# Between two scans: channels split 128 and 64, means through GpSimd, convolution by halves

## The chip, the cores and the metric

The kernel runs on one core of a Trainium2 chip. The metric is the device time of one execution in microseconds; a version's time is the median of its runs. For the kernel before it is 23751.5 us (three runs, 23744.67 to 23764.05). Times inside the kernel come from one profiled execution.

## The reference

The input is x with eight images of 64 x 64 positions and 192 channels, all fp32. Two layers follow each other. Each normalises its input by groups of channels and adds its result to it. The change lies in the second one:

```
x = x + L1(gn(x))
L1:  xc, z = split(x @ in_proj.T)            # 384 channels each
     xc = silu(depthwise_conv3x3(xc) + b)
     xs = xc by rows, by columns, and both reversed        # 4 directions
     dt, B, C = xs @ x_proj ;  delta = softplus(dt @ dt_proj + bias)
     h = exp(delta * A) * h + delta * B * xs ;  y = sum_n h * C     # scan over 4096 positions
     y = sum of the four directions + xs * D
     y = layernorm(y) * silu(z) ;  return y @ out_proj.T
```

## The kernel before, in words

Layer 0 comes first, for all images, and leaves its result channel-major in DRAM (x1s). Layer 1 (function layer1) then takes one image after the other. Positions go in eight tiles of TT = 512 (eight rows of the image); the 384 inner channels are DT = 3 groups of 128 partitions; the 192 outer channels are CT = 2 groups of CP = 96 partitions.

The scan of an image (function scan, its part main) is written out in a fixed order and is not touched. Between the scan of image b-1 and that of image b stands a boundary, which does two things side by side: the finish of image b-1, and the front of image b with the prologue of its scan. The loop over b at the end of layer1 runs nine times: the first boundary has only a front, the last only a finish.

The front (function front) loads a tile of x1s, projects it with p_x (L1141, two matmuls that add over the two groups of 96 channels) into a PSUM bank, copies it with a bias into a padded image (pad, L1171), and convolves: ScalarE writes tap 0 (L1192), VectorE adds taps 1 to 8 with scalar_tensor_tensor in place over the whole image, 128 x 4096 (L1202). Then ScalarE applies SiLU by halves (L1215) and writes the result three ways to DRAM: by channels (L1220), transposed by columns (xt, L1230 and L1234), and by tokens (by_tokens: four TensorE transposes p_xq, a copy xq, a DMA; L1249 to L1261). When all is written, the prologue may load (xc, ut; L1462 and L1466), project (p_d), make the step widths (spa, de), transpose (p_du) and weigh (pw, L1592); then decays ea and transposes g feed the first scans.

The finish (function finish) works on yacc, the sum of the four directions, which stays in SBUF as 128 x 3 x 4096. By tile: the mean over 384 channels is three matmuls with a matrix of 1/384 (p_m, L1281), VectorE subtracts it (L1289), ScalarE squares (L1299), three matmuls give the variance (p_v, L1281), ScalarE takes logarithm and exponential (L1317, L1318), VectorE multiplies (L1324), ScalarE scales and shifts by group (L1331). Beside it z is projected from a reloaded tile of x1s (p_z, L1361) and goes through SiLU (L1379); VectorE multiplies (L1391), p_o projects to 192 channels (L1408), VectorE adds the input (L1417), and a DMA stores.

The order on each engine is not written by hand. The class Flow is a planner: each piece of front and finish is a generator of steps with an engine, a guessed cost and buffers to take and give. At each turn Flow issues the step that could start first by its guesses (a rank breaks ties), and keeps that order on every engine with order-only dependencies. The guesses never reach the chip; the order does. Two waits are thus to be kept apart: a generator's wait orders the plan, while on the chip an engine runs its queue in order and waits by semaphores for data and buffers. All DMAs are issued by SP.

PSUM in a boundary: five banks mm (means, p_z, p_o, prologue), two banks fx (p_x, p_xq), one outside. SBUF buffers: two xl1, two xs, one xt, two xq; three xl2, two z, one square. The scan's own buffers h1 (hs, hc) take memory that the finish leaves.

Of the kernel before, what the change touches and what calls it, by code (L numbers as in the profile page):

```python
# [8 lines left out]
F32 = mybir.dt.float32  # L9
# [84 lines left out]
class Flow:  # L94
# [48 lines left out]
    def start(self, req, ready):  # L143
# [3 lines left out]
        if req[0] == "take":  # L147
            return (-1.0, max(ready, min(self.slots[req[1]]))) if self.slots[req[1]] else None
# [6 lines left out]
    def run(self):  # L155
        while self.chains:
# [8 lines left out]
            if req[0] == "take":  # L165
                self.slots[req[1]].remove(min(self.slots[req[1]]))
# [866 lines left out]
def layer1(tc, consts, x1s, mv1, out, w_in, w_x, w_dt, w_out):  # L1033
# [5 lines left out]
    image = lambda ap: ap.rearrange("(t p) l -> p t l", p=CP)  # L1039

    with ExitStack() as ctx:
# [8 lines left out]
        wi = wp.tile([CP, CT, 2 * DIN], F32, name="wi1")  # L1050
        nc.sync.dma_start(out=wi, in_=w_in.rearrange("(t p) m -> p t m", p=CP))
# [25 lines left out]
        sc, sh = gn_affine(tc, sp, mp, mv1.rearrange("p b t s -> p (b t) s"), grp, eps)  # L1077
        pb = mp.tile([128, TT], F32, name="p_gb", tag="mm")
        for m in range(2 * DT):
            for ct in range(CT):  # L1080
                nc.tensor.matmul(
                    pb[:, m * nb : m * nb + nb],
                    wi[:, ct, m * 128 : m * 128 + 128],
                    sh.rearrange("p (b t) -> p b t", t=CT)[:, :, ct],
                    start=ct == 0,
                    stop=ct == 1,
                )
# [5 lines left out]
        def scaled(w, b, half):  # L1093

            for ct in range(CT):
# [5 lines left out]
                            w[:, ct],  # L1101
                            wi[:, ct, half * DIN : half * DIN + DIN],
                            AF.Copy,
                            scale=sc[:, b * CT + ct : b * CT + ct + 1],
# [5 lines left out]
        def front(f, cx, mq, b, xo):  # L1110


            fp = cx.enter_context(tc.tile_pool(name="fr1", bufs=1, reuse_waits="tile"))
            wx_b = fp.tile([CP, CT, DIN], F32, name="wx1b")
            pads = [fp.tile([128, HI + 2, WI + 2], F32, name=f"pad{i}") for i in range(2)]
            for tag, n in (("xl", 2), ("fx", 2), ("pad", 2), ("xs", 2), ("xt", 1), ("xq", 2)):
# [3 lines left out]
            def load():  # L1120
                for d in range(DT):
                    for t in range(NT):
                        tk = slice(t * TT, t * TT + TT)
                        yield "take", "xl"
                        xl = got["xl", d, t] = fp.tile([CP, CT, TT], F32, name="xl1", bufs=2)
                        r = yield step("SP", 0.1, lambda: [nc.sync.dma_start(out=xl, in_=image(x1s[b])[:, :, tk])])
                        f.at["xl", d, t] = r + 3

            def project():
                yield from scaled(wx_b, b, 0)  # L1130
                for d in range(DT):
                    for t in range(NT):
                        yield "wait", ("xl", d, t)
                        xl = got["xl", d, t]
                        yield "take", "fx"
# [758 lines left out]
```

## Time and profile before

| what | us |
|---|---|
| median of three runs | 23751.5 |
| profiled execution, its own time | 23759.13 |
| its span | 23757.4 |
| first stretch without a scan (front alone) | 196.2 |
| seven boundaries with front and finish | 251.3, 248.6, 248.0, 247.2, 248.1, 248.5, 248.6 |
| last stretch (finish alone) | 135.5 |
| a scan between two boundaries (5070.0 to 7173.6) | 2103.6 |

A stretch is counted from the end of one scan's last hc (L1648 on GpSimd) to the start of the next scan's first. The profile's page has one line per group of instructions: line, engine, operation, output and inputs with shapes, count; then busy time and mean duration, and the idle time of the engine just before them with what ended it. In a table of stretches each engine has its busy microseconds and, in brackets, its instructions; then come the granted clock of TensorE, the share of the DMA engines, and GB/s. An fp32 matmul stands in the trace as two instructions.

### The profile page before, as it was taken

How to read it: one execution, taken by the hardware profiler on the slowest of the kernel's cores; microseconds unless marked ns; L12 is line 12 of the kernel's file. 1: busy time of each engine (PE TensorE's matmuls, PEld its weight loads, DVE VectorE, ACT ScalarE, POOL GpSimd, SP SyncE). 2: the span in 40 equal slices, each digit the busy share in tenths (PEclk: the TensorE clock that was granted, in tenths of full speed). 3: DMA queues.
4: the chain of work that ended last, by engine and by line, in shares of the span. 5: the costliest groups of instructions: out<-in, count | busy, mean ns of one | idle time of the engine just before them, and what ended most of it. 6: DMA issues, size and time to landing. Idle time of an engine off the chain costs nothing.

```text
span 23757.4 us, 313126 instructions
## 1 busy us (share of the span) xinstructions
PE 21089.6 (89%) x100804; PEld 10279.5 (43%) x100804; DVE 21274.2 (90%) x22093; ACT 21040.0 (89%) x37507; POOL 16067.4 (68%) x12871
## 2 busy tenths in 40 slices
PE   7999999978888888888888888888888888888888
PEld 4444444434444444444444444444444444444444
DVE  7888888779998999899989998999899989998998
ACT  5666766669998999899989998999899989998998
POOL 1111111149995999599959985998699769976997
PEclk8999999989999999999999999999999999999999
DMA  2111111133233323333233233323332233233332
GB/s 50 45 44 44 46 44 43 39 99 81 81 79 107 81 82 78 107 81 82 76 112 81 82 77 109 81 81 79 110 82 81 78 107 82 81 85 100 82 83 67
DMA packets 1368290, 1859.75 MB, mean 78 GB/s; under 512 B 268576, under 2 KB 697024, under 8 KB 1357440
## 3 DMA queue, kind: packets, MB, share of 16 engines
q1 hardware_dynamic: 1366656, 1839.73, 28.7%
q8 instruction: 810, 13.27, 0.2%
q14 instruction: 824, 6.75, 0.1%
HBM read 1225.98 MB, written 210.50 MB: 60 GB/s over the span
## 4 chain that ended last, share of the span: by engine, by line
POOL 43%; PE 24%; ACT 15%; DVE 7%; issue 6%; DMA 4%; SPq 1%; POOLq 0%; ACTq 0%; DVEq 0%
POOL hc L1648 40%; ACT pw L1592 6%; ACT ea L1607 6%; POOL cy L1646 3%; PE p_f L956 3%; DMA xc<-xo 2%; DVE xs L1202 2%; PE p_f L976 2%; PE p_x L448 2%; PE y L1663 2%; PE p_o L873 2%; PE p_y L790 1%; PE g L1618 1%; PE p_d L1481 1%; PE p_z L531 1%
## 5 line engine op out<-in xcount | busy, mean ns | idle before, releaser
L1648 POOL TENSOR_TENSOR hc<-hs,cb 128x1024 f32<-128x1024 f32 x6144 | 14592.9, 2375 | 12.0 <-POOL cy L1646 9.9
L1634 DVE TENSOR_TENSOR_SCAN hs<-ea,cy,g 128x512 f32<-128x512 f32 x10752 | 13024.0, 1262 | 608.6 <-PE g L1618 411.1
L1592 ACT ACTIVATE pw<-duT,bt 128x384 f32<-128x384 f32 x16384 | 8874.1, 601 | 20.2 <-DVE duT L1539 20.2
L1607 ACT ACTIVATE ea<-dr,an 128x512 f32<-128x512 f32 x12288 | 8120.5, 709 | 189.2 <-DVE hs L1634 170.8
L1663 PE MATMUL y<-hc,sel 128*64 128x512 f32 x24576 | 6624.0, 617 | 1841.3 <-POOL hc L1648 1819.2
L1618 PEld LDWEIGHTS g<-ident,pw 128*128 128x128 f32 x49152 | 5288.7, 141 | 4336.8 <-issue 2671.4
L1618 PE MATMUL g<-ident,pw 128*128 128x128 f32 x49152 | 6788.4, 279 | 60.1 <-ACT pw L1592 28.6
L1646 POOL COPY cy<-hs 128x2 f32<-128x2 f32 x6144 | 1164.2, 189 | 3373.5 <-DMA out_x<-xl 1733.8
L1663 PEld LDWEIGHTS y<-hc,sel 128*64 128x64 f32 x24576 | 1225.9, 134 | 3254.1 <-POOL hc L1648 3031.3
L1634 DVE TENSOR_TENSOR_SCAN hs<-ea,g 128x512 f32<-128x512 f32 x1536 | 1763.7, 1202 | 159.0 <-PE g L1618 115.6
L365 POOL TENSOR_TENSOR s<-xs 96x512 f32<-96x512 f32 x64 | 121.1, 1892 | 2033.7 <-DVE xs L343 1522.9
L1202 DVE SCALAR_TENSOR_TENSOR xs<-pad,p,xs 128x4096 f32<-128x4096 f32 x192 | 860.9, 4484 | 43.4 <-ACT xs L1192 36.2
L1510 PE MATMUL p_dt<-xdbl,wd 13*128 13x512 f32 x1536 | 857.2, 639 | 41.0 <-DVE de L1523 39.1
L365 POOL TENSOR_TENSOR s<-sq 96x512 f32<-96x512 f32 x128 | 211.6, 1653 | 964.1 <-ACT sq L378 899.8
L1481 PE MATMUL p_d<-xc,wx 128*44 128x512 f32 x1536 | 791.6, 598 | 22.6 <-DMA xc<-xo 22.0
L343 DVE SCALAR_TENSOR_TENSOR x<-xx,p,x 96x512 f32<-96x512 f32 x1024 | 785.2, 815 | 19.4 <-ACT x L332 19.4
L956 PE MATMUL p_f<-h,wf 96*128 96x512 f32 x1536 | 761.9, 632 | 24.4 <-ACT zs L550 14.0
L343 DVE SCALAR_TENSOR_TENSOR xs<-xin,p,xs 96x512 f32<-96x512 f32 x1024 | 749.3, 767 | 4.6 <-ACT xs L332 4.6
L976 PE MATMUL p_f<-m,wf 128*96 128x512 f32 x1536 | 692.9, 601 | 0.0
L1532 PEld LDWEIGHTS p_du<-ident,de 128*128 128x128 f32 x3072 | 323.5, 141 | 610.2 <-DVE de L1523 405.8
L448 PE MATMUL p_x<-h,wi 96*128 96x512 f32 x1024 | 544.5, 664 | 12.3 <-ACT h L405 11.1
L365 POOL TENSOR_TENSOR s<-x 96x512 f32<-96x512 f32 x64 | 96.2, 1502 | 626.3 <-DVE x L343 477.2
(202 smaller groups left out, 19557.2 us busy)
## 6 DMA issues: line engine op xcount, KB each, us to landing
cb<-cd SPq DMA_DIRECT2D x4096, 128.0 KB
dr<-de SPq DMA_DIRECT2D x3072, 128.0 KB
xc<-xo SPq DMA_DIRECT2D x256, 768.0 KB
e<-csd SPq DMA_DIRECT2D x256, 384.0 KB
xl<-x SPq DMA_DIRECT2D x256, 384.0 KB
ut<-xo SPq DMA_DIRECT2D x128, 768.0 KB
ut<-xo SPq DMA_DIRECT2D x256, 384.0 KB
xo<-xs SPq DMA_DIRECT2D x48, 1024.0 KB
```

The source lines that it names most:

```text
L343: nc.vector.scalar_tensor_tensor(im(out[:, ct]), tap(ct, j), w[:, ct, j : j + 1], im(out[:, ct]), ALU.mult, ALU.add)
L956: nc.tensor.matmul(ps, wf1[:, ct, mt * 128 : mt * 128 + 128], h[:, ct], start=ct == 0, stop=ct == 1)
L976: nc.tensor.matmul(ps[:CP], wf2[:, kt, ct * CP : ct * CP + CP], m[:, kt], start=kt == 0, stop=kt == 5)
L1202: nc.vector.scalar_tensor_tensor(xs, tap(j), kw[:, d, j : j + 1], xs, ALU.mult, ALU.add)
L1481: nc.tensor.matmul(st["p_d"][:44], wx[:, d, k], st["xc"][:, d], start=d == 0, stop=d == DT - 1)
L1592: nc.scalar.activation(st["pw", p, j][:, :, i], st["duT"][:, j].rearrange("p (g c) -> p g c", c=64), AF.Copy, scale=st["bt"][:, j, n : n + 1],
L1607: nc.scalar.activation(ea[:, f], state[s]["dr", d][:, f], AF.Exp, scale=an[:, k, p, at : at + 1])
L1618: nc.tensor.transpose(g[:, f, j * 128 : j * 128 + 128], state[s]["pw", p, j][:, 2 * d + f].rearrange("p a b -> p (a b)"), ident,)
L1634: nc.vector.tensor_tensor_scan(rev(h[:, f]), rev(ea[:, f]), rev(g[:, f]), 0.0 if first(s) else state[s - 1]["cy"][:, p, d, f : f + 1], ALU ...
L1646: o(nc.gpsimd.tensor_copy(st["cy"][:, p, d], h[:, :, last]))
L1648: o(nc.gpsimd.tensor_mul(hc, h, bc(st["cb", p], 1, [128, 2, TT])))
L1663: o(nc.tensor.matmul(y[half[f]], sel, hc[:, f], start=p == 0 and k > 0, stop=p == NP1 - 1))
```

## The change

It rewrites the boundary and leaves layer 0 and the scan alone.

- Outer channels are held as 128 partitions and 64 (twice, once on each half of the partitions) instead of 96 and 96. Two tiles of 512 go together: a load is three DMAs (parts), a projection is pair: two matmuls over 128 channels, then two over 64 channels, one on each half of the array's rows. The output projection does 128 columns a tile, and the other 64 columns of both tiles side by side on halves of the array's columns (rest). Scale and shift of the group norm are moved to that layout through DRAM once (affd, aff).
- The mean over 384 channels: GpSimd adds the three groups (two additions of 128 x 512 into ys, one buffer), then one matmul instead of three.
- The convolution runs in two halves of 32 rows with three xs buffers; SiLU, stores, tokens and the transposing copy follow by halves.
- PSUM: mm has three banks, p_z two of its own (zz). A pair of p_x takes both fx banks, a pair of p_z both zz banks.
- The plan: LATE makes centre and gate wait, from tile 4 on, for the first tap of the last convolution's halves; every chain has a rank, LAG is 0.35 and RANK 1.0; a take may ask for several buffers.
- The softplus of the step widths (spa: exp, then ln with a bias of 1) is the same in both files.

```diff
+    def parts(ap, xl, t):
+        two = ap.rearrange("c (t l) -> c t l", l=TT)[:, t : t + 2]
+        return [(xl[:, 0:2], two[0:128])] + [(xl[i * 64 : i * 64 + 64, 2], two[128:C, i]) for i in range(2)]
+    def pair(w, m, ps, xl):
+        out = [nc.tensor.matmul(ps[i], w[:, 0, m], xl[:, i], start=True, stop=False) for i in range(2)]
+        for i in range(2):
+            rows = slice(i * 64, i * 64 + 64)
+            out.append(nc.tensor.matmul(ps[i], w[rows, 1, m], xl[rows, 2], start=False, stop=True))
+        return out
...
+        affd = dp.tile([C, 2, nb], F32, name="affd", bufs=1)
+        aff = wp.tile([128, 2, 2, nb], F32, name="aff")
+        for i, a in enumerate((sc, sh)):
+            for ct in range(CT):
+                nc.sync.dma_start(
+                    out=affd[ct * CP : ct * CP + CP, i], in_=a.rearrange("p (b t) -> p t b", t=CT)[:, ct]
+                )
+        nc.sync.dma_start(out=aff[:, 0], in_=affd[0:128])
+        for i in range(2):
+            nc.sync.dma_start(out=aff[i * 64 : i * 64 + 64, 1], in_=affd[128:C])
...
             def convolve():
                 for d in range(DT):
-                    yield "wait", ("pad", d)
-                    xs = got["xs", d] = fp.tile([128, HI, WI], F32, name="xs1", bufs=2)
-                    tap = lambda j: pads[d % 2][:, j // 3 : j // 3 + HI, j % 3 : j % 3 + WI]
+                    for h in range(2):
+                        yield "wait", ("pad", d, h)
+                        xs = got["xs", d, h] = fp.tile([128, HI // 2, WI], F32, name="xs1", bufs=3)
+                        at = h * HI // 2
+                        tap = lambda j: pads[d % 2][:, at + j // 3 : at + j // 3 + HI // 2, j % 3 : j % 3 + WI]
...
-                    xt = fp.tile([128, WI, HI], F32, name="xt1")
-                    r = yield step("ACT", 7.2, lambda: [nc.scalar.copy(xt, xs.rearrange("p h w -> p w h"))])
+                            lambda: [nc.scalar.copy(xt[:, :, at : at + HI // 2], xs.rearrange("p h w -> p w h"))],
...
-            def mean(ps, src):
-                return [nc.tensor.matmul(ps, on, src[:, d], start=d == 0, stop=d == DT - 1) for d in range(DT)]
+            def mean(src):
+                yield "take", "ys"
+                ys = fp.tile([128, TT], F32, name="ys", bufs=1)
+                yield step(
+                    "POOL",
+                    2.6,
+                    lambda: [nc.gpsimd.tensor_add(ys, src[:, 0], src[:, 1]), nc.gpsimd.tensor_add(ys, ys, src[:, 2])],
+                )
+                yield "take", "mm"
+                ps = mq.tile([128, TT], F32, name="p_m", tag="mm")
+                r = yield step("PE", 1.0, lambda: [nc.tensor.matmul(ps, on, ys, start=True, stop=True)])
+                f.give("ys", r)
+                return ps, r
             def centre():
                 for t in range(NT):
+                    if (t in LATE) and b + 1 < nb:
+                        yield "wait", ("tail", LATE[t])
...
+                    def rest():
+                        for d in range(DT):
+                            for i in range(2):
+                                f.keep(
+                                    nc.tensor.matmul(
+                                        pr[i * 64 : i * 64 + 64],
+                                        wo[:, d, 128:C],
+                                        yacc[:, d, tk(t + i)],
+                                        start=d == 0,
+                                        stop=d == DT - 1,
+                                    )
+                                )
...
-            f.STAY = 0.0
+            f.LAG, f.STAY, f.RANK = 0.35, 0, 1.0
-            mq = mq_x.enter_context(tc.tile_pool(name="mq1", bufs=5, space=PSUM, reuse_waits="tile"))
-            f.pool("mm", 5)
+            mq = mq_x.enter_context(tc.tile_pool(name="mq1", bufs=3, space=PSUM, reuse_waits="tile"))
+            f.pool("mm", 3)
```

## The prediction

> **What bounds the kernel now.** I read the page first, then the engines' busy time by stretch, then the chain of waits through one boundary, then the rows of single operations. The page says that all engines are nearly full over the span, and that the chain is GpSimd's; that is the scan, which the change doesn't touch.
>
> ```profile
> span 23757.4 us, 313126 instructions
> PE 21089.6 (89%) x100804; PEld 10279.5 (43%) x100804; DVE 21274.2 (90%) x22093; ACT 21040.0 (89%) x37507; POOL 16067.4 (68%) x12871
> L1202 DVE SCALAR_TENSOR_TENSOR xs<-pad,p,xs 128x4096 f32<-128x4096 f32 x192 | 860.9, 4484 | 43.4 <-ACT xs L1192 36.2
> ```
>
> So I cut the span at the scan's first and last multiplication by C (hc, L1648). Between the scans stand nine stretches: the first (front of image 0 alone), seven in which the finish of one image runs beside the front of the next, and the last (finish alone). Columns: length, busy time by engine, clock, DMA.
>
> ```profile
> 4873.80:5070.00 196.20, 97.17 (x261) 47.77 (x261) 115.10 (x36) 88.45 (x85) 0.91 (x5) 0.68 0.53 167
> 14226.30:14473.50 247.20, 210.56 (x528) 91.37 (x528) 166.49 (x76) 154.04 (x170) 0.82 (x5) 0.90 0.49 153
> 23621.90:23757.40 135.50, 128.10 (x292) 52.99 (x292) 53.65 (x41) 65.22 (x81) 0.00 (x0) 0.97 0.17 47
> ```
>
> The seven are 247.2 to 251.3 us, together 1740; with the other two 2072, 8.7% of the span. All of the forecast lies there. The fifth boundary, cut where its convolution begins and ends on VectorE:
>
> ```profile
> 14226.30:14270.10 43.80, 43.73 (x104) 19.18 (x105) 16.22 (x11) 29.62 (x34) 0.82 (x5) 1.00 0.40 109
> 14270.10:14387.60 117.50, 94.85 (x236) 41.29 (x234) 116.56 (x33) 68.21 (x66) 0.00 (x0) 0.88 0.51 167
> 14387.60:14473.50 85.90, 71.98 (x190) 30.90 (x190) 33.72 (x35) 56.21 (x71) 0.00 (x0) 0.86 0.52 156
> ```
>
> Three stages, three limits: TensorE for 43.8 us (43.73 busy), VectorE for 117.5 us (116.56 busy, of which 24 taps at 4.48), and an 85.9 us tail in which no engine is full. The chain of waits tells what the tail is:
>
> ```profile
> 14393.12 6.58 DMA xo<-xq
> 14401.12 8.71 DMA xo<-xq
> 14418.36 6.33 DMA xc<-xo
> 14456.72 13.45 PE p_o L1408 x24
> ```
>
> Token copies wait for their writes, the next image's first load waits for them, and at the end four output projections of the old image stand in TensorE's queue ahead of the new image's first transposes.
>
> **What the Trainium skill says.** "SBUF — State Buffer", section on the two separate sides: a VectorE operation with two SBUF inputs and a GpSimd operation that reads SBUF take one port pair as an exclusive lock, for the whole instruction. The trace agrees. In layer 0, five taps (L343) run while one GpSimd addition runs; then six without:
>
> ```profile
> L343 DVE SCALAR_TENSOR_TENSOR x<-xx,p,x x5: 736/736/1746, 4532.0 to 4535.7; 96x512 f32<-96x512 f32 x5
> L365 POOL TENSOR_TENSOR s<-sq x1: 1283/1283/1283, 4533.2 to 4533.2; 96x512 f32<-96x512 f32 x1
> L343 DVE SCALAR_TENSOR_TENSOR xs<-xin,p,xs x6: 739/740/741, 4519.8 to 4524.5; 96x512 f32<-96x512 f32 x6
> ```
>
> One tap lasted 1746 ns instead of 736: one addition cost VectorE 1.01 us. "GPSIMD Engine Reference", Engine selection, advises VectorE for elementwise work; no run here puts the same addition on both. "TensorEngine Tiling (Array Packing)", Key Properties: tiles work in parallel, and a change of the tiling mode drains the array. For tiles of 64 columns the trace agrees:
>
> ```profile
> 14474.54 1.08 PE L1661 MATMUL y<-xc,dskip 128*64 128x512 f32 x4
> 14241.22 1.88 PE L1141 MATMUL p_x<-xl,wx1b 96*128 96x512 f32 x4
> ```
>
> Four passes on two tiles end after 1.08 us, four full ones after 1.88 (in the chain of waits they count 1.72, 0.43 each). Tiles of 64 rows it doesn't show. A pass is half an fp32 matmul, so a matmul of 512 columns is 0.86 us.
>
> **Part by part, for a full boundary.**
>
> TensorE. Projections p_x and p_z: 12 pairs each, four matmuls (3.44) become two full and two half ones side by side (2.58 and two mode changes, 0.1 each by the gap before the y row): 0.66 less, 24 times, 15.8. If row tiles don't overlap: 0.2 more each, 4.8 lost. Output projection: 12 matmuls a pair of tiles become 6 and 6 side by side, 9 in time: 2.4 less, 4 times, 9.6. Means: 16 times three matmuls become one: 27.5. In all 53 us less, but TensorE is the limit only in the start and the last stretch.
>
> Start (43.8 now). TensorE passes nine means of three matmuls and eight tiles of p_x before the pad is full; now half a pad is enough (tiles 0 to 4, three pairs). In the changed order these are three pairs of p_x, two means and two pairs of p_z: 5 x 2.8 + 2 x 0.86 = 15.7, and the first p_z must wait for its load, issued behind two others at about +2 and, at the 222 GB/s of this stretch, landed near +9 instead of +5. With the last two pads (1.4) and the first tap on ScalarE (1.9) VectorE starts at 25. Gain 19.
>
> Middle (117.5 now). This is VectorE's sum. Taps: 48 halves. Starts are now 4.52 apart, of which 4.27 is 4096 elements at 0.96 per ns and 0.25 the wait for the tap before; so a half is 2.39, and 48 are 114.7 against 108.5. Other work: 2 of the 24 operations of 1.75 (1.67 apart) lie in the start and 6 in the tail by the changed order, so 16 are inside, 26.7 us, and six additions of 0.61, 3.7; now only 9 us are inside. That is not extra work: it was done in the start and the tail, where it was free. The lock: 32 additions of 128x512 on GpSimd are new. About seven fall before the taps; 25 lie in them, at 1.01 each 25.3. Bounds: 0 (each in a gap) and 32 x 1.27 = 41. I take 25, for VectorE's queue is without gaps here and about nine in ten of its microseconds have two SBUF inputs. Sum 114.7 + 26.7 + 3.7 + 25.3 = 170.4; loss 53.
>
> Tail (85.9 now). After the last half tap: SiLU and table load 3.5, transposing copy of a half 3.7 instead of 7.3, old-image work in ScalarE's order 4; the 2 MB write of xt goes out at about +8 and the last four token writes queue behind it as they do now (6.6 and 8.7): last copy at +22, not +30. Then load of xc 6.3 and p_d 3.4, an output projection 2.6 and the copy: +35. From that copy to the first hc the first stretch, undisturbed, takes 17 (5052.8 to 5070.0); one more output projection adds 3. Tail 55; gain 31. The final output projections now stand before the weights are ready.
>
> Boundary: 25 + 170.4 + 55 = 250.4 against 247.2: 3 us more. Seven: +22.
>
> First stretch: scale and shift are bounced through DRAM, two DMAs in a row; by "SBUF — State Buffer", DMA setup, about 2 us each, with six issues of 0.4 an estimate of +7, before the weights can be scaled. Half a pad saves about 15 of the 33 before the first tap; taps +6; in the tail four token writes and half a transposing copy less, -10. Sum -12. No GpSimd means here.
>
> Last stretch: TensorE busy 128.1 of 135.5. Without 32 matmuls of means (27.5), 12 x 0.66 and 9.6 it is 83; the means' GpSimd additions (16 x 2.5) overlap, but the chain mean, square, mean, logarithm, product is longer by them, so I take 100. Sum -35.
>
> PSUM: the general banks fall from five to three, p_z has two of its own. Prologue and output projections share the three, so in the tail p_du waits for a bank that de or an addition frees: in the 3 above, between 0 and 6. A pair of p_x takes both fx banks, so it waits for two copies to the pad (1.4); TensorE has room for that except in the first stretch, where it is counted. A pair of p_z waits for two SiLUs, and the means behind it wait too; I put this at nothing while VectorE has taps queued, else it is up to 2 a pair. The first stretch, with TensorE half idle, was granted a clock of 0.68; if less work lowers it here, the tail's matmuls cost some 2 more. The waits for the tail mark in centre and gate only shape the written order; no instruction waits on them.
>
> SP issues 60 input and output DMAs instead of 40 a boundary, at 0.3 to 0.4: 7 us, in a queue that mostly waits for buffers. ScalarE's sums stay.
>
> Total 22 - 12 - 35 = -25 us. The profiled execution took 23759.1 (span 23757.4), 7.6 above the median; on the median 23751.5 it gives 23726.
>
> **Rivals.** *The lock is mild:* additions run during the centring operations (one input is PSUM) or in gaps, and the scheduling moves p_m earlier. For it: the order puts additions beside centring. Against it: the 1746 ns. With 8 additions charged and a tail of 52 a boundary is 230: 7 x -18 - 47 = -170, 23580. *Slower, a wait in place of the port:* the order is planned with 2.6 us for a mean, but an addition waits for a tap of 2.35 first, so a mean takes 2 x (1.2 + 1.2) to 2 x (2.35 + 1.2), 4.8 to 7.1; there is one ys buffer, and the second half's eight means are one file through GpSimd. 2 to 4.5 us late, eight times, VectorE waits in order at its centring and normalising operations, with taps queued behind: about 20 a boundary, +161 - 47 + 5 = 120: 23870. It decides once the means are over 2.6 us late where the plan left no slack. *It doesn't do what it says:* the softplus is unchanged in the diff (exp and ln stood apart already), and row tiles may not overlap: 24 x 0.86 a boundary on TensorE, about 6 of them in start and tail, 10 in the last stretch: +50 on the sum, no change.
>
> **How the numbers follow.** The sum has 0.45 (own range 23660 to 23790), the mild lock 0.22, the late means 0.28, the tiles 0.05. 0.2% is 47 us, about what a measurement of this kernel can tell from no change: beyond 23704 or 23799. The sum gives faster 0.18, same 0.22, slower 0.05; the mild lock faster 0.22; late means slower 0.27, same 0.01; tiles same 0.04, slower 0.01. Together 0.40, 0.27, 0.33. Range 23560 to 23880: it takes in the mild lock and most of the late means.
>
> **What would show it.** Right: taps of about 2.35 us of which some twenty a boundary last 3.3; the middle near 170, the start near 25, the tail near 55, boundaries within 10 of 248, the last stretch near 100. Wrong if taps stay at 2.35 beside GpSimd, if VectorE idles more than 15 us between taps, or if the first load of xc comes later than 30 us after the last tap.

## The result, and the profile after

Slower: 23835.5 us (median of six runs, 23806.79 to 23847.79) against 23754.78 for the kernel before on the same chip (six runs). The ratio is 1.0033, with a 95% interval of 1.0023 to 1.0043, so about 80 us more. The profiled execution took 23847.79 us and is the longest of its six, 12 above their median.

The page of the kernel after: its span, the engines, and the two groups that the change made. A group's columns are busy time and mean duration, then the idle time of the engine before it and what ended that.

```profile
span 23846.1 us, 312719 instructions
PE 20808.6 (87%) x100292; PEld 10075.4 (42%) x100292; DVE 21404.2 (90%) x22253; ACT 21057.9 (88%) x37573; POOL 16523.3 (69%) x13127
L1227 DVE SCALAR_TENSOR_TENSOR xs<-pad,p,xs 128x2048 f32<-128x2048 f32 x384 | 978.2, 2548 | 139.9 <-ACT xs L1215 107.8
L1322 POOL TENSOR_TENSOR ys<-yacc 128x512 f32<-128x512 f32 x64 | 115.3, 1802 | 694.4 <-PE p_m L1326 694.4
```

TensorE is busy for 281 us less and the kernel is longer. VectorE gained 130 us of busy time; a half tap takes 2548 ns in the mean, while its median in the fifth boundary is 2352. GpSimd idled 694 us before its additions, and what ended that was always p_m, the matmul that frees the one buffer ys.

The table of stretches for the same fifth boundary (start, middle and tail, cut where the convolution begins and ends on VectorE) and for the last stretch. Columns as before: length, busy time by engine, TensorE's clock, DMA share, GB/s.

```profile
14261.70:14287.30 25.60, 23.88 (x58) 7.72 (x58) 4.20 (x3) 11.10 (x14) 10.39 (x12) 0.88 0.77 197
14287.30:14459.00 171.70, 107.93 (x286) 40.23 (x282) 158.08 (x71) 106.71 (x112) 50.94 (x25) 0.78 0.41 136
14459.00:14515.30 56.30, 39.68 (x125) 15.86 (x126) 21.64 (x23) 33.09 (x45) 0.18 (x2) 0.82 0.58 179
23706.40:23846.10 139.70, 104.50 (x228) 34.06 (x228) 56.55 (x37) 68.48 (x83) 46.57 (x33) 0.82 0.15 45
```

The middle lasts 171.7 us with VectorE busy 158.1. Before, 0.9 us of it was idle; now it is 13.6 (in the mean of the seven boundaries 16.4, for 2.0 before). The waits that the view lists for VectorE here (engine, what waited, what ended it, us in total, times, longest):

```profile
DVE xs L1227 <- DMA xl<-x: 7.3, 1, 7.3
DVE xs L1227 <- ACT xs L1215: 7.0, 1, 7.0
DVE yacc L1336 <- PE p_m L1326: 5.3, 2, 3.3
```

The first, 7.3 us, ended with the first tap itself at 14287.3, so it lies in the start. The other two make 12.3 us of the middle's idle time. How the longest wait for p_m comes about stands in the timeline (start, duration, engine, line; in brackets the idle time before it and what ended that):

```profile
14423.08 3.23 DVE L1227 SCALAR_TENSOR_TENSOR xs<-pad,p,xs 128x2048 f32<-128x2048 f32 x1
...
14424.25 3.20 POOL L1322 TENSOR_TENSOR ys<-ys,ysq 128x512 f32<-128x512 f32 x1
...
14427.50 2.08 PE L1326 MATMUL p_m<-ys,on 128*128 128x512 f32 x2 [3.96 <-POOL ys L1322]
...
14429.66 3.38 POOL L1322 TENSOR_TENSOR ys<-yacc 128x512 f32<-128x512 f32 x1 [2.21 <-PE p_m L1326]
...
14433.11 3.19 POOL L1322 TENSOR_TENSOR ys<-ys,yacc 128x512 f32<-128x512 f32 x1
...
14436.36 2.07 PE L1326 MATMUL p_m<-ys,on 128*128 128x512 f32 x2 [6.79 <-POOL ys L1322]
...
14438.48 1.75 DVE L1336 TENSOR_TENSOR yacc<-yacc,p_m 128x1536 f32<-128x1536 f32 x1 [3.29 <-PE p_m L1326]
```

The mean for centring can't begin before the matmul of the variance has read ys (14429.6). From there two additions of 3.3 us, each held up by a tap, and a matmul of 2.1 (1.1 in the start of the same boundary) make 8.8 us; the plan had counted 2.6 and 1.0. VectorE stands at its centring operation, with taps behind it.

The 7.0 us before the first tap of the fourth half have another chain. ScalarE writes tap 0 (L1215) behind copies xq that waited for token writes to free their buffers, and behind a copy to the pad that waited for a pair of p_x:

```profile
14365.63 1.28 ACT L1289 COPY xq<-p_xq 128x512 f32<-128x512 f32 x2 [8.30 <-DMA xo<-xq]
...
14374.43 0.69 ACT L1191 ACTIVATE pad<-p_x,gb 128x512 f32<-128x512 f32 x1 [4.30 <-PE p_x L1052]
14375.02 2.08 ACT L1215 ACTIVATE xs<-pad,p 128x2048 f32<-128x2048 f32 x1
```

No mean stands in this chain. Over the seven boundaries the waits for p_m come to 5.5 us each in the middle, those for tap 0 to 8.4.

Means over the seven boundaries, for both kernels and the runs that follow. "Head" is the time from a scan's first hc to its ninth. It belongs to the boundary: a scan that starts before ScalarE has a lead makes up for it in its first units. "First" runs from the group norm's last matmul to the first hc, "last" from the last hc to the end. The medians come from different chips; the kernel before, measured beside each, lay between 23754.8 and 23760.1 there, and the ratios given with the experiments compare on one chip.

| kernel | start | middle | tail | boundary | head | first | last | median |
|---|---|---|---|---|---|---|---|---|
| before | 44.1 | 118.6 | 86.1 | 248.7 | 23.0 | 197.5 | 135.5 | 23754.8 |
| after | 25.5 | 174.3 | 56.6 | 256.4 | 27.5 | 206.2 | 139.6 | 23835.5 |
| before_halves | 30.0 | 137.8 | 74.4 | 242.2 | 22.6 | 198.2 | 134.8 | 23684.6 |
| before_means_gp | 34.3 | 130.4 | 96.5 | 261.2 | 22.5 | 197.8 | 122.5 | 23813.5 |
| means_te | 23.7 | 143.4 | 60.3 | 227.5 | 23.6 | 206.4 | 132.6 | 23605.2 |
| means_te_spin | 22.9 | 158.7 | 61.8 | 243.4 | 23.0 | 206.1 | 137.3 | 23716.6 |
| after_sq_inplace | 25.5 | 162.1 | 57.1 | 244.7 | 26.0 | 203.7 | 136.1 | 23755.4 |
| after_plan_guess | 25.6 | 157.8 | 73.3 | 256.6 | 22.6 | 204.0 | 147.2 | 23832.5 |
| te_old_plan | 23.8 | 129.2 | 97.3 | 250.3 | 22.5 | 206.7 | 134.3 | 23766.8 |
| te_aff_xl4 | 23.9 | 143.3 | 60.7 | 228.0 | 23.3 | 189.0 | 124.2 | 23587.9 |
| te_late_half | 24.3 | 141.6 | 64.5 | 230.5 | 25.1 | 189.1 | 124.6 | 23618.6 |
| gp_repaired | 25.1 | 161.8 | 57.0 | 244.0 | 26.8 | 189.0 | 126.7 | 23737.4 |
| gp_warm | 26.1 | 162.1 | 57.1 | 245.3 | 26.3 | 188.7 | 129.8 | 23737.4 |

Where the 88.7 us between the two spans went: the boundaries 7 x 7.7 = 54, the scans 28 (the heads after the seven boundaries account for it, 4.4 each), the first stretch 8.7, the last 4.1. Layer 0, which is the same program, was 5.6 us shorter in this execution. The head shows in the waits of the kernel after from the end of this boundary on; the line below it is from the same place in the kernel before:

```profile
DVE hs L1708 <- PE g L1692: 7.2, 3, 2.9
PEld g L1692 <- ACT pw L1666: 5.8, 5, 1.7
```

```profile
ACT ea L1607 <- DVE hs L1634: 15.1, 3, 12.7
```

The first scans wait for the transposes g, and those for weights of ScalarE, which runs without a pause from 14506.9, in the tail, into the scan. Before, ScalarE had rested 12.7 us in one piece there, its weights done, while the last output projections ran. So the tail is 61 us rather than 57: of the 29.5 us that it gained at the first hc, 4.4 are given back.

The first stretch: the timeline from the group norm to the scaled weights.

```profile
4867.85 0.91 SPq L1099 DMA_DIRECT2D affd<-gn_sc  x2
4868.86 1.64 SPq L1099 DMA_DIRECT2D affd<-gn_nb  x2
4886.14 0.34 SPq L1102 DMA_DIRECT2D aff<-affd  x1
4886.53 1.10 SPq L1104 DMA_DIRECT2D aff<-affd  x2
4888.86 1.12 ACT L1127 ACTIVATE wx1b<-wi,aff 128x384 f32<-128x384 f32 x2 [21.03 <-DMA aff<-affd]
```

Four pieces of 3 KB were written; 16 us after the last of these issues the wait for them ended (SP waited 15.4 us) and they were read back, which took under 3; the weights are scaled 22 us after the group norm's matmul instead of 1. The pieces go out as packets of 4 bytes: from 4870.5 to 4876.5 the DMA engines were 0.91 busy and moved 1 GB/s, and then nothing moved until 4886.1. What fills these ten us no run shows.

The last stretch: three lines of its waits, then the chain of waits near its end and two equal groups of matmuls.

```profile
DVE yacc L1336 <- PE p_m L1326: 33.7, 8, 8.7
POOL ys L1322 <- PE p_m L1326: 32.7, 14, 5.5
DVE yacc L1438 <- ACT z L1425: 19.7, 2, 16.9
```

```profile
23808.21 2.38 DMA out_x<-xl
23810.73 4.71 DMA xl<-x
23815.49 3.78 PE p_z L1049 x4
...
23825.86 1.99 PE p_z L1049 x4
23827.85 1.11 PE p_z L1052 x4
```

Two things run one after the other here that ran side by side before: the means, and the last pair's load, which needs the buffer of the second pair and so its output. And the same four passes of p_z last 3.78 us just after TensorE had waited and 1.99 ten microseconds later. The granted clock was 0.73 to 0.89 in this stretch (0.97 before).

### The profile page after: what moved, and what is told of

The parts are those of the page before. It is cut to its first block, busy times and chain, and to the rows that moved or that the text cites. A ratio compares the mean times of both kernels' runs of the same rounds, so it can differ in the third digit from the quotient of the medians.

```text
span 23846.1 us, 312719 instructions
## 1 busy us (share of the span) xinstructions
PE 20808.6 (87%) x100292; PEld 10075.4 (42%) x100292; DVE 21404.2 (90%) x22253; ACT 21057.9 (88%) x37573; POOL 16523.3 (69%) x13127
## 4 chain that ended last, share of the span: by engine, by line
POOL 44%; PE 23%; ACT 14%; DVE 7%; issue 6%; DMA 3%; SPq 1%; POOLq 0%; ACTq 0%; DVEq 0%
POOL hc L1722 41%; ACT pw L1666 6%; ACT ea L1681 6%; POOL cy L1720 3%; PE p_f L957 3%; DVE xs L1227 2%; PE p_f L977 2%; DMA xc<-xo 2%; PE p_x L449 2%; PE y L1737 2%; PE p_o L874 2%; PE p_y L791 1%; PE g L1692 1%; PE p_d L1555 1%; PE p_z L532 1%
## 5 line engine op out<-in xcount | busy, mean ns | idle before, releaser
L1722 POOL TENSOR_TENSOR hc<-hs,cb 128x1024 f32<-128x1024 f32 x6144 | 14583.4, 2374 | 12.7 <-POOL cy L1720 11.5
L1227 DVE SCALAR_TENSOR_TENSOR xs<-pad,p,xs 128x2048 f32<-128x2048 f32 x384 | 978.2, 2548 | 139.9 <-ACT xs L1215 107.8
L366 POOL TENSOR_TENSOR s<-sq 96x512 f32<-96x512 f32 x128 | 206.7, 1615 | 963.1 <-ACT sq L379 892.1
L344 DVE SCALAR_TENSOR_TENSOR x<-xx,p,x 96x512 f32<-96x512 f32 x1024 | 784.7, 814 | 15.4 <-ACT x L333 15.4
L1322 POOL TENSOR_TENSOR ys<-yacc 128x512 f32<-128x512 f32 x64 | 115.3, 1802 | 694.4 <-PE p_m L1326 694.4
```

The source lines that it names most:

```text
L344: nc.vector.scalar_tensor_tensor(im(out[:, ct]), tap(ct, j), w[:, ct, j : j + 1], im(out[:, ct]), ALU.mult, ALU.add)
L1227: nc.vector.scalar_tensor_tensor(xs, tap(j), kw[:, d, j : j + 1], xs, ALU.mult, ALU.add)
L1722: o(nc.gpsimd.tensor_mul(hc, h, bc(st["cb", p], 1, [128, 2, TT])))
```

## The experiments

**1. What the means on GpSimd cost, and by what.** The main theory was that they are the whole loss, half by the shared port and half by the wait for the mean. The first run puts the three matmuls back into the kernel after; the second adds GpSimd's additions to it again, with nobody waiting for them.

```diff
 means_te
-                yield "take", "ys"
-                ys = fp.tile([128, TT], F32, name="ys", bufs=1)
-                yield step(
-                    "POOL",
-                    2.6,
-                    lambda: [nc.gpsimd.tensor_add(ys, src[:, 0], src[:, 1]), nc.gpsimd.tensor_add(ys, ys, src[:, 2])],
-                )
                 yield "take", "mm"
...
-                r = yield step("PE", 1.0, lambda: [nc.tensor.matmul(ps, on, ys, start=True, stop=True)])
-                f.give("ys", r)
+                r = yield step(
+                    "PE",
+                    2.8,
+                    lambda: [nc.tensor.matmul(ps, on, src[:, d], start=d == 0, stop=d == DT - 1) for d in range(DT)],
+                )
...
 means_te_spin, in addition, after each centring
+            def spin(src, r):
...
+                yield step(
+                    "POOL", 5.2, lambda: [nc.gpsimd.tensor_add(ys, src[:, i], src[:, i + 1]) for i in (0, 1, 0, 1)], r
+                )
...
+                    f.fork(spin(yv, r))
```

> The kernel after with the means as three matmuls on TensorE again; all else stays. Theory A (the GpSimd means are the loss: about 15 us of port lock and 5 to 10 us of waits for p_m in each middle, and the serial means with a cold TensorE in the last stretch): start 25.5 rises to about 29, middle 174 falls to about 155, tail 56 stays; a boundary falls from 256 to about 241, the last stretch from 139.6 to 120, the whole by 7 x 15 + 20 = 125 to about 23710. Theory B (the loss is the order of the plan and the stall at the fourth half, the means cost nothing): middle 170 or more, boundary 254 to 260, last stretch 125 to 140, the whole 23800 to 23850.

> Means on TensorE as in the run beside it, and after each centring four GpSimd additions of 128x512 whose result nobody reads (as many as the GpSimd means make). Only the shared port is left of the GpSimd means, no wait for them. Theory lock: the middle is 12 to 16 us above the run without these additions (a dozen taps of 3.3 and centring and normalising operations of 2.7 instead of 1.75). Rival (the lock is mild, what costs is the wait for the mean): within 4 us of it.

Measured: means_te 23605.2 us, 0.9936 of the kernel before (0.9921 to 0.9951); means_te_spin 23716.6 us, 0.9983 (0.9976 to 0.9990). The middle of the fifth boundary in both (means_te first), and the taps of the second there (shortest, median and longest in ns):

```profile
14200.70:14345.10 144.40, 117.02 (x328) 46.53 (x328) 138.96 (x68) 112.13 (x119) 0.00 (x0) 0.94 0.45 151
```

```profile
14235.20:14394.70 159.50, 123.36 (x327) 48.70 (x328) 153.98 (x68) 112.37 (x119) 57.20 (x20) 0.86 0.41 137
L1227 DVE SCALAR_TENSOR_TENSOR xs<-pad,p,xs x48: 2341/2352/3358, 14235.1 to 14392.3; 128x2048 f32<-128x2048 f32 x48
```

Theory A holds: the means are more than the whole loss (a boundary came to 227.5 for its 241). Only the last stretch gained less than it said, 132.6 for 120.

The port costs 15.9 us a boundary (243.4 - 227.5), as theory lock said: 14 taps of 48 last 3.0 to 3.4 us instead of 2.35, and three of the other operations 2.5 to 2.8 instead of 1.75. Of GpSimd's 20 additions in this stretch 17 last 2.7 to 3.2 us instead of 1.27: it waits for the port as well. The kernel after has the same cost in its own trace: in the fifth middle, 14 taps and four other operations are longer, by 16.4 us together. Its eight centring operations, which take one input from PSUM, never lengthen (0.08 us together), though each had a GpSimd addition beside it.

From means_te_spin to the kernel after there are 13.0 us a boundary and 4.5 in the head left. Seven times 17.5 is 123, and the medians differ by 119. These are the waits for the means, together with the other order that the plan wrote around such means. Tail and head together are the same in both (84.8 and 84.1), so the loss lies in the start (2.7) and the middle (15.6). In the middle VectorE idles 11.7 us more: 5.5 before centring operations, for p_m, and 6 before first taps. The rest, 3.9, is other work that now falls into the middle.

**2. Each half of the change in the kernel before.**

```diff
 before_halves (front as in the kernel after, for 96 and 96 channels)
+                    for h in range(2):
+                        yield "wait", ("pad", d, h)
...
+                        xs = got["xs", d, h] = fp.tile([128, HI // 2, WI], F32, name="xs1", bufs=3)
...
 before_means_gp (mean as in the kernel after)
-                    q = yield step("PE", 2.8, lambda: mean(pm, yv), 0.0)
+                    pm, q = yield from mean(yv)
```

> The kernel before with one part of the change: the convolution in two halves, with stores, tokens and the transposing copy by halves. My prediction's terms, applied here: the start 44 falls to about 33 (five tiles of p_x instead of eight), the middle 118.6 rises to 48 x 2.39 + about 14 x 1.67 + 4 = 142, the tail falls from 86 to about 58; a boundary 233, 15 less than before; the first stretch 196 falls to 172; the whole 23754 - 7 x 15 - 24 = 23625. Rival (order of the planner without its new ranks puts old work ahead of the front, so that what the tail gains the middle loses): boundary 245 to 255, the whole 23720 to 23760.

> The kernel before with one part of the change: the means as two GpSimd additions and one matmul. Theory A: TensorE's start gets shorter (44 to about 34), the middle grows by lock and waits (118.6 to about 138), the tail stays at 86; a boundary 258, 9 more than before, the last stretch 140, the whole about 23830. Rival (means are cheaper on GpSimd where TensorE bounds): start 30, middle 122, boundary 238, the whole 23680.

Measured: the halves 23684.6 us, 0.9969 (0.9957 to 0.9980). A boundary became 6.5 us shorter instead of 15 and ended, at 242.2, between theory (233) and rival (245): start (30.0 for 33) and middle (137.8 for 142) came out better than worked out, but the tail kept 74.4 instead of 58. In the first stretch nothing was gained: its start and its tail became 10 and 11 us shorter, but its convolution took 131 us for 109, since VectorE there waits 16 us for the first taps of the halves. The means 23813.5 us, 1.0024 (1.0015 to 1.0032): slower, as theory A said, but not by its stages. The start gains 10 us as it said; the middle loses 12 instead of 19, and the tail, which has more of the old image's work left, loses 10 where it had nothing. The last stretch came to 122.5 instead of 140: with three small buffers xl2 the means on GpSimd do relieve it. The loss by the means needs neither the halves nor the pairs; the gain in the last stretch was there and the pairs took it away.

**3. One buffer, or the order?** In the kernel after, the squares' sum is made in the square's own buffer, so that ys serves the centring alone; or the plan is told that a mean's additions take twice as long.

```diff
 after_sq_inplace
-            def mean(src):
+            def mean(src, ys=None):
...
+                own = ys is None
+                if own:
+                    yield "take", "ys"
+                    ys = fp.tile([128, TT], F32, name="ys", bufs=1)
...
-                    got["pv", t], r = yield from mean(sq)
+                    got["pv", t], r = yield from mean(sq, sq[:, 0])
...
 after_plan_guess
                     "POOL",
-                    2.6,
+                    5.2,
```

> The kernel after, with one edit: the sum of the squares is made in the square's own buffer, so that only the centring means take ys. Theory one-buffer (the 17 us a boundary that separate the kernel after from the run with idle additions come from the single ys buffer): VectorE's idle time in the middle falls from 14.8 to about 5, the middle from 174 to about 163, a boundary from 256 to 245, the last stretch from 139.6 to 130, the whole by 75 us or more. Rival (the length of the chain addition, addition, matmul itself, or the copies of xq in ScalarE's order, make them): the middle stays above 170 and the whole within 30 us of the kernel after.

> The kernel after, with one number of the plan changed: a mean's two additions are guessed at 5.2 us instead of 2.6; the work is the same and only the order on the engines changes. Theory guess (the mean comes later than the plan thinks, and VectorE meets its centring too early): idle time of VectorE in the middle falls from 14.8 to 5, a boundary to 246. Rival (the order is not what makes them late): middle 172 to 176, boundary 253 to 259.

Measured: 23755.4 us with the second place for a sum, 0.9997 (0.9989 to 1.0006), the time of the kernel before; 23832.5 with the other guess, 1.0032 (1.0020 to 1.0043), the time of the kernel after. The waits of VectorE in the fifth middle of after_sq_inplace, all of them (the third lies before the first tap):

```profile
DVE yacc L1441 <- ACT z L1428: 2.1, 1, 2.1
DVE xs L1227 <- ACT xs L1215: 0.6, 1, 0.6
DVE xs L1227 <- DMA xl<-x: 0.5, 1, 0.5
DVE yacc L1372 <- ACT yrs L1366: 0.4, 1, 0.4
```

Over the seven boundaries VectorE's idle time in the middle fell from 16.4 to 5.3 us: no wait for p_m is left, and those for tap 0 fell from 8.4 to 0.6. So the one-buffer theory forecast the sizes rightly. The cause isn't parted, though: the plan also writes another order when a buffer is free. The other guess changes the order and leaves the buffer. It too nearly ends both waits (p_m 1.1, tap 0 0.2), so for the wait at tap 0 another order is enough. But it gained nothing: the middle fell to 157.8, below what its rival said, the boundary stayed at the rival's 253 to 259, and the time moved into the tail:

```profile
14278.60:14435.90 157.30, 95.46 (x266) 38.04 (x264) 147.75 (x65) 97.23 (x98) 40.07 (x18) 0.77 0.42 140
14435.90:14509.20 73.30, 50.23 (x143) 19.86 (x144) 32.28 (x29) 50.06 (x66) 12.94 (x11) 0.85 0.48 149
```

GpSimd's additions are now in the tail too (12.9 us). With the one buffer kept, this order saved nothing; that no other could, no run shows.

**4. The order.** Means on TensorE as in means_te, but planned as before the change.

```diff
-        LATE = {4: 0}
+        LATE = {}
...
-            f.LAG, f.STAY, f.RANK = 0.35, 0, 1.0
+            f.STAY = 0.0
...
-                f.chain(gen, rank)
+                f.chain(gen)
```

> Means on TensorE, and the order planned as before the change: no ranks by chain, no wait for the mark of the last convolution, the old lag. Work, tiles and buffers are those of the run with means on TensorE. Theory order (what that run gains over the halves alone, 242 to 227 a boundary, is the order, above all the shorter tail): a boundary 238 to 244, the tail 72 or more. Rival (it is the pairs of tiles, 25 us less on TensorE): a boundary 226 to 232.

Measured: 23766.8 us, 1.0001 (0.9992 to 1.0010). The fifth boundary:

```profile
14230.60:14255.40 24.80, 24.76 (x56) 9.27 (x57) 5.97 (x5) 12.22 (x15) 0.80 (x4) 0.88 0.81 210
14255.40:14384.50 129.10, 94.71 (x272) 38.08 (x270) 126.57 (x60) 86.91 (x88) 0.00 (x0) 0.88 0.51 170
14384.50:14482.40 97.90, 73.57 (x203) 29.01 (x204) 36.71 (x34) 54.74 (x74) 0.15 (x2) 0.85 0.35 111
```

The order is worth 23 us a boundary (250.3 to 227.5), more than the 11 to 17 that the theory had. The middle is shorter without it, because old work is left lying, and the tail then carries it: TensorE is busy 73.6 of its 97.9 us. Without the new order, halves and pairs together gain nothing on the kernel before. The halves alone do (242.2, experiment 2), so in the old order the pairs, with their fewer buffers and banks, cost 8 us a boundary; which part of them costs it, no run shows.

**5. First and last stretch.** Scale and shift reach the new layout by matmuls with pieces of the identity instead of through DRAM, and the last stretch alone has four pair buffers. Then the marks for the old image's second half put later still.

```diff
 te_aff_xl4
-        affd = dp.tile([C, 2, nb], F32, name="affd", bufs=1)
...
-                nc.sync.dma_start(
-                    out=affd[ct * CP : ct * CP + CP, i], in_=a.rearrange("p (b t) -> p t b", t=CT)[:, ct]
-                )
...
+                    nc.tensor.matmul(
+                        pa[:, at : at + nb],
+                        shift[:, j, ct],
+                        a.rearrange("p (b t) -> p t b", t=CT)[:, ct],
+                        start=ct == cts[0],
+                        stop=ct == 1,
+                    )
+        nc.vector.tensor_copy(aff.rearrange("p j i b -> p (j i b)"), pa[:, : 4 * nb])
...
+            XB = 2 if b + 1 < nb else 4
...
+                    xl = got["xl2", t] = fp.tile([128, 3, TT], F32, name="xl2", bufs=XB)
...
 te_late_half, in addition
-        LATE = {4: 0}
+        LATE = {4: 1}
```

> Means on TensorE, and two edits that touch different stretches. First: scale and shift reach the layout of 128 and 64 by matmuls with a shifted identity instead of DMAs through DRAM; this should take 14 to 17 us from the first stretch (206 to about 190, measured from the group norm's last matmul) if the bounce is what made it longer, none if something else did. Second: the last stretch alone has four pair buffers xl2 instead of two; theory load (the last pair's load waits for the output of the second pair): last stretch 132.6 falls to about 120; rival (TensorE's own 114 us and the chain at its end bind): 128 or more. The boundaries stay at 227 in both. The whole: 23605 - 15 - 10 = 23580 with the theories, 23600 without.

> Means on TensorE, scale and shift by matmuls, four xl2 in the last stretch (as te_aff_xl4), and the old image's tiles 4 to 7 planned after the first tap of the last half instead of the last but one. The middle is VectorE's sum (48 taps 112.8 and 30 us of other work) and the tail has VectorE mostly idle. Theory cover (old work moved from the middle to the tail is free there): the middle 143 falls to about 133, the tail stays near 62, a boundary 219, the whole 23530. Rival (the tail has no room: its TensorE and ScalarE queues carry the rest of that work ahead of the new image's transposes): what the middle gains the tail loses, a boundary 226 to 232.

Measured: te_aff_xl4 23587.9 us, 0.9929 (0.9914 to 0.9944), the lowest median of all; te_late_half 23618.6, 0.9939 (0.9922 to 0.9956). These intervals and that of means_te overlap, so the lengths of the stretches have to tell the three apart. The first stretch fell from 206.4 to 189.0, the last from 132.6 to 124.2:

```profile
23460.10:23584.30 124.20, 114.02 (x292) 43.21 (x292) 50.65 (x38) 62.99 (x79) 0.00 (x0) 0.97 0.18 51
```

The bounce is what made the first stretch longer, as its theory said. The load has a part in the last one: 124.2 lies between its theory (120) and the rival (128). Old work put later takes 1.7 us from the middle and gives 3.8 to the tail and 1.8 to the head: the tail has no room for it, as the rival said.

**6. Is it the clock?** The kernel after with all three repairs (squares in place, scale and shift by matmuls, four xl2 in the last stretch), and the same with two matmuls more behind each mean's of the last stretch, so that TensorE idles less.

```diff
 gp_warm
-                r = yield step("PE", 1.0, lambda: [nc.tensor.matmul(ps, on, ys, start=True, stop=True)])
...
+                    lambda: [nc.tensor.matmul(ps, on, ys, start=True, stop=True)]
+                    + [nc.tensor.matmul(warm, on, idle, start=True, stop=True) for _ in range(2 if b + 1 == nb else 0)],
```

> The kernel after with three repairs, the means still on GpSimd: squares summed in their own buffer, scale and shift by matmuls, four xl2 in the last stretch. Theory: first stretch 189 (measured from the group norm's last matmul), boundaries 245, last stretch 136 falls to about 122 since the load of the last pair no longer waits for an output; the whole 23755 - 17 - 14 = 23725. Rival (in the last stretch the chain of GpSimd and TensorE binds, not the load): last stretch 132 to 136.

> As gp_repaired, and in the last stretch alone two more matmuls behind each mean's, into a PSUM bank that nobody reads: as much TensorE work as means on TensorE would be, without their place in the chain. Theory clock (TensorE runs at half pace after idling, and this made the last stretch miss my 100): its clock in the last stretch goes from about 0.8 to above 0.93 and the stretch gets 3 to 10 us shorter in spite of 27 us of extra work. Rival (the clock is no limit; the chain is): the stretch stays within 2 us, or grows by up to 10.

Measured: both 23737.4 us, 0.9991 (0.9983 to 1.0000 and 0.9982 to 0.9999). In gp_repaired the first stretch (189.0) and the boundaries (244.0) came as its theory said; the last stretch took 126.7 us, 9.4 less than with two xl2 (136.1), between theory (122) and rival (132). With all three repairs the means on GpSimd still cost 150 us against the same repairs with means on TensorE (te_aff_xl4): 16.0 us a boundary and 3.6 in the head. Most of it is the port, 15.9 in experiment 1.

With the added matmuls the last stretch took 129.8. Its second and third 30 us in both, gp_repaired first:

```profile
23651.00:23681.00 30.00, 19.71 (x38) 6.51 (x38) 16.76 (x12) 17.84 (x23) 22.69 (x15) 0.78 0.09 26
23681.00:23711.00 30.00, 23.41 (x48) 7.71 (x48) 9.99 (x7) 19.90 (x26) 2.53 (x2) 0.77 0.03 10
```

```profile
23637.60:23667.60 30.00, 28.89 (x73) 11.82 (x72) 20.81 (x12) 19.43 (x24) 24.95 (x16) 1.00 0.05 18
23667.60:23697.60 30.00, 25.76 (x59) 9.60 (x58) 12.90 (x9) 23.69 (x31) 5.08 (x4) 0.94 0.04 9
```

The clock did rise, from 0.78 and 0.77 to 1.00 and 0.94, and the other matmuls were busy for 88 us instead of 97.5, yet the stretch got no shorter. So the theory, as it was put, falls. The test isn't clean, though: the added matmuls took 33 us in TensorE's own queue and left it idle for only 13, so what a higher clock without them would be worth stays open. Likeliest is the chain of means, logarithms and products, for which TensorE idles 29 us in gp_repaired; which link of it would have to go to reach 100 us is open. In the boundaries the clock wasn't tried: there too it is lower with the means on GpSimd (0.78 in the fifth middle, 0.94 in means_te), and what that adds to the waits no run shows.

## Why the prediction was wrong

It said 23726, with faster likelier than slower; measured is 80 us slower. What failed is the step that put VectorE's waits at nothing: the sum has taps, other work and port, but no wait for a late mean. Without this step's 17.5 us a boundary the kernel is faster than before, in spite of all other errors (means_te_spin, 23716.6). The next is the last stretch. The time lies near the rival of late means (23870, put at 0.28). Its mechanism, VectorE standing at its centring operations behind one ys buffer, is in the trace, but the nearness is in part luck: the rival had the boundaries 161 us longer (measured, heads included, 85) and the first and last stretch together 47 shorter (measured 13 longer). By the steps:

- **Start 25, middle 170.4, tail 55** came to 25.5, 174.3 and 56.6. The three stages were seen rightly; in the start the load of p_z landed at +9.4, for the 9 taken. The sum for VectorE without GpSimd was right too: 114.7 + 26.7 + 3.7 = 145.1, and means_te has 143.4. Its 0.96 elements per ns come out of the two lengths of tap that the prediction shows, 4484 ns for 4096 and 739 for 512. That the 0.25 us beside it are the wait for the tap before, no run shows. The middle as a whole, though, is near by two errors that offset each other, the next two.
- **The lock, 25.3 us**, measured 15.9 in means_te_spin and about 16 in the kernel after. The price of one meeting was right (1.01 us there, 0.9 here); the count was not. I took 25 of 32 additions as charged. In the kernel after 24 lie in the middle, but only 18 VectorE operations are longer, since additions also fall beside centring operations and into gaps.
- **Waits, put at nothing in the sum**: measured 13.0 us in the boundary and 4.5 in the head, +123 us in all, of which the lock's error gives 66 back. I had worked out the mean's 4.8 to 7.1 us in the rival and then kept it out of the sum, because VectorE's queue seemed full enough to hide it. It isn't hidden: VectorE works in order, so a late mean stops the taps that are queued behind it (5.5 us a boundary at centring). About as much again stands before tap 0 of the fourth half. There the prediction had seen that a pair of p_x takes both fx banks and had put the wait at nothing, because TensorE has room; but tap 0 waits for it. Which share of this second part the means make, and which the order, stays open (experiment 3).
- **Tail**: right at the first hc, but I stopped counting there. Some 4.4 us went over into the scan's head, 31 us in all; with them the tail is 61. That is no wait for the means: means_te has 60.3 and a head of 23.6. The head is counted in the 17.5 as well, so the two items can't be added.
- **First stretch, -12**, measured +8.7. The half pad (-11.6 for my -15) and the tail (-10.8 for -10) held; the taps cost 10.1 for 6. The bounce was the error: 21 us for 7. My estimate took about 2 us for each DMA from the Trainium skill ("SBUF — State Buffer", DMA setup); here the write of small pieces held the reading up for 16 us, so that figure doesn't fit such pieces. The matmuls in te_aff_xl4 took 17.4 us off.
- **Last stretch 100**, measured 139.6: 39 us, the largest error of one stretch. TensorE's work with the means on TensorE was right: the sum gives 128.1 - 8 - 9.6 = 110, and means_te has 113.8. Without them it was 104.5 for my 83, at a clock of 0.82 instead of 0.97 (88 in gp_warm, at 0.95). And TensorE no longer set the end. The runs took off 3.5 us by the second place for a sum and 9.4 by the load's buffers; 126.7 are left, 27 above my 100, of which TensorE works 97.5 and waits for the chain in the rest. I hadn't asked how soon two pair buffers come free when each is also the output.
- **That it doesn't do what it says** falls for the tiles: the four half-row passes of p_z take 1.11 us where four full ones take 1.99. This agrees with "TensorEngine Tiling (Array Packing)", Key Properties.
- **The signs named ahead**: VectorE idling more than 15 us between taps was one for wrong, and it came: 16.4 in the mean, if 13.6 in the fifth boundary. Of those for right, start, middle, tail and boundary came within what was said (256.4 is within 10 of 248), and the last stretch didn't.

## What to carry to other kernels

Work moved from a full engine to an idle one is priced by what it makes others wait for: here the means' matmuls (27.5 us a boundary on TensorE by the prediction's sum, little of it on the path) were paid for with 16 us a boundary of port and 17 of waits, behind one small buffer and in the order planned around it. Before costing a longer chain at nothing, look which in-order queue its result is waited for in, what is queued behind that instruction, and how many buffers the chain goes round in. A stage's end is where the next one runs at its full pace, not where its first instruction starts.

## What the runs showed of the hardware

- A GpSimd addition of 128x512 beside VectorE operations with two SBUF inputs lasts 2.7 to 3.2 us instead of 1.27 (means_te_spin), and the VectorE operation about 0.9 longer. Beside taps of twice the length (before_means_gp) such additions last 4.4 to 5.3 us, and the taps 5.37 instead of 4.48, again 0.9 longer: the price of one meeting didn't grow with the tap. VectorE's centring operations, with one input from PSUM, never lengthened.
- TensorE's passes of 512 columns took about twice their time just after it had idled (four p_z passes 3.78 us after 3.5 us of idle time, against 1.99). Filling it with unread matmuls brought the clock back, but no time.
- Four DMAs of 3 KB from 96 partitions to DRAM, in packets of 4 bytes, were waited for until 16 us after the last issue; the DMA engines moved nothing in the last ten of these. Reading 16 KB back took under 3.
- Layer 0, the same program in all these kernels, ended between 4856 and 4887 us from the span's start in their profiles. A difference of 15 us between two whole executions says little on the boundaries; their own lengths, seven in each profile and mostly within 5 us of each other, say more. For the same reason a kernel's stretches don't add up to the difference of medians better than to some 20 us.
